# Hyperedge attention in a four-layer graph kernel: score products, closing steps and loads of two chunks issued together

## The chip, the cores and the metric

The kernel runs on one core of a Trainium2 chip. The metric is the device time of one execution in microseconds (us), and lower is better. The figure for a kernel is the median of several executions.

The core has five engines with instruction queues of their own, each worked off in order: PE (matrix multiplication; its weight loads, PEld, run beside the multiplications), DVE (element-wise work and reductions), ACT (activation functions), POOL (element-wise work, and here mostly the issuing of DMAs) and SP (which only issues DMAs). They meet at semaphores. [...]

## The reference, cut to what matters

Four graph layers are computed one after the other on `x` of shape (8, 2048, 64), each as `x = x + layer(relu(layernorm(x)))`. The change touches the end of the first, an attention over hyperedges. When that end begins there are two candidates for every node, `industry` (neighbours averaged through `adj`) and `g` (hyperedges averaged by attention), and a softmax over the two mixes them:

```python
def attn_scores(f):
    return jnp.tanh(f @ fcW + fcb) @ av
...
pair = jnp.stack([industry, g], axis=2)
coefs2 = jax.nn.softmax(attn_scores(pair), axis=-1)
out = jnp.einsum('bnk,bnkf->bnf', coefs2, pair)
```

A softmax over two scores is a sigmoid of their difference d, and a sigmoid is `0.5 + 0.5*tanh(d/2)`. So the kernel computes `tanh(fcW' industry + fcb) - tanh(fcW' g + fcb)`, multiplies by `av`, takes `tanh(d/2)`, and blends `g + (tanh(d/2) + 1) * (industry - g)/2`. The second layer, an attention over neighbours, follows at once.

## The kernel before, in words

`four_layers` (line 2299) runs `layer0`, then `Layer1`, then layers 2 and 3. The last part of `layer0` (lines 1500 to 1593), here called **the mixing stage**, is what the change touches. Two batches lie side by side on the 128 partitions, so there are four pairs p of batches, and each has 2048 nodes in four chunks of 512 columns: 16 chunks, numbered 0 to 15. Chunks 0 to 3 belong to p = 0.

The steps of chunk i, and the engine of each:

- `fetch(i)` (line 1520): SP loads `industry` of the chunk into one of eight buffers `iv`. Chunk i takes the buffer of chunk i - 8, and so waits until that chunk is finished and stored.
- `first(i)` (1525) and `second(i)` (1528): through `scores` (1509) PE multiplies `fcW` with `industry` (named `iv`) or with `g` (named `hn` in the trace, `gT` in the code) into a two-bank PSUM tile `pf`. ACT takes the tanh of it into an SBUF tile `th_s`. There are two `pf` tiles, so a product has to wait for the tanh of the product two before it. `second` also has DVE turn `iv` into the half difference of the candidates.
- `differ(i)` (1534): DVE subtracts the two tanh tiles (128 by 1024).
- `third(i)` (1537), "the score product": PE multiplies `Av` with that difference into a one-bank tile `pd`, and ACT takes the tanh in place. There are two `pd` tiles, so the product of a chunk needs `fourth` of the chunk two before it to have read its tile.
- `fourth(i)` (1545), "the closing step": DVE blends into `iv`. For p = 0 two more additions on DVE follow (1552, 1553), and SP stores the sum; for the other p, POOL issues a DMA that adds `iv` to `x1_dram`. After the last chunk of each p, `late_tile` has POOL load one more tile of the adjacency matrix.

The order on each engine is written out by hand. `InOrder` (line 624) and `kit.mm` with `kit.strict` (735) keep each instruction where the program puts it on its engine. The loop from line 1572 runs i from 0 to 17; turn i of it issues, in this order, `first(i + 1)`, `second(i + 1)`, `third(i - 1)`, `differ(i)`, `fourth(i - 2)` and `fetch(i + 6)`, each where its chunk exists.

Between them, `near(engine, i)` issues pieces of the next layer for p = 0 (`first_neighbours`, line 1667, with its plan from line 1771). The ones that matter here are the means (`centre`, two chunks in turns 4 and 8, PE), the subtraction of them (`centred`, turns 5 and 9, DVE), `clipped` on DVE, `maps` (turns 6, 7, 10 and 11, PE, into tiles `ph`), the 13 small DVE operations `guess`, `newton` and `scored` (turns 12 and 13), `rows` (turns 14 and 15, PE, into `pb`), and four products `edge` (turns 16 and 17, DVE, 128 by 1024 each, named `pt`). With these `edge` tiles the attention over neighbours starts: `Layer1.attend` (line 1821), whose DVE products are on line 1813 and whose PE products are named `o` and `dn`.

In the trace, instructions issued through `kit.mm` have line 737, and those through `InOrder` have line 632, so they are told apart by tile.

## Time and profile before

| | us |
|---|---|
| median of 3 runs (lowest, highest) | 1865.65 (1864.99, 1867.82) |
| the profiled execution | 1868.58 |
| its span | 1866.8 |
| PE busy in the span | 1826.9 (98%) |
| DVE busy | 1196.0 (64%) |
| ACT busy | 476.1 (26%) |
| POOL busy | 317.9 (17%) |
| first product of the mixing stage (PE, `pf`) | at 351.46 |
| first DVE product of `attend` (line 1813) | at 421.95 |

All times "at" are counted from the start of the span. The profiled execution took 1.8 us more than its span, and 2.9 us more than the median. In a timeline a row gives its start, its duration, the engine, the line, the operation, what it writes and reads, the shape, and how many instructions were merged; in square brackets stands how long the engine had been idle before it and what ended that. In a list of waits a row gives who waited for whom, the sum in us, how often, and the longest. In a table by stage a row gives the stretch, its length, the busy time of each engine (with its number of instructions), the granted PE clock as a share of full speed, and the load of the DMA engines.

### The profile page before, as it was taken

Reading aid. Unit: us, or ns where it says so; the run is one execution under the profiler, and the core shown is the slowest. Engines: PE = TensorE matmul, PEld = TensorE weight load, DVE = VectorE, ACT = ScalarE, POOL = GpSimd, SP = SyncE. Lnnn points to the kernel's source line nnn. Section 1 sums busy time; section 2 is a strip of 40 time slices with the busy share of each in tenths; the row PEclk is TensorE's granted clock in tenths of the full one; section 3 lists DMA queues with packets and bytes.
Section 4 is the critical chain, followed back from the end, with each engine's and each line's share of the span. In section 5 each row is a group of like instructions: output and inputs, shape, how many; then the busy total and the mean of one; then the engine's idle time right before and its main releaser. Section 6 shows DMA issues by size and latency. Waiting matters only on the chain.

```text
span 1866.8 us, 26248 instructions
## 1 busy us (share of the span) xinstructions
PE 1826.9 (98%) x10358; PEld 1137.9 (61%) x10358; DVE 1196.0 (64%) x1881; ACT 476.1 (26%) x1088; POOL 317.9 (17%) x437
## 2 busy tenths in 40 slices
PE   7999999899999999999999999999999999999997
PEld 7878767343333333477765577855677755777653
DVE  6778799789999998932446722367533276424465
ACT  5433455672222221121301112201112101113000
POOL 3212487120000000000112200012100021101122
PEclk9999999999999999999999999999999999999998
DMA  6677494492222222142101022100122011221000
GB/s 189 167 211 221 126 280 127 118 215 75 60 54 56 51 57 58 46 104 64 51 10 31 22 70 62 34 24 25 44 63 63 12 29 29 62 57 51 5 20 13
DMA packets 84390, 142.61 MB, mean 76 GB/s; under 512 B 31752, under 2 KB 32008, under 8 KB 81520
## 3 DMA queue, kind: packets, MB, share of 16 engines
q1 hardware_dynamic: 62832, 79.59, 14.6%
q0 software_dynamic: 21200, 58.03, 12.8%
q10 hardware_dynamic: 224, 3.22, 0.5%
q8 instruction: 83, 1.36, 0.3%
q14 instruction: 51, 0.42, 0.1%
HBM read 106.85 MB, written 37.09 MB: 77 GB/s over the span
## 4 chain that ended last, share of the span: by engine, by line
PE 50%; issue 10%; DMA 2%; POOL 2%; DVE 1%; POOLq 0%; ACT 0%; SPq 0%; DVEq 0%
PE acc L737 31%; PE u L737 14%; PE py L737 2%; PE pv L737 1%; PE tx L744 1%; PE tv L744 1%; POOL fold L2284 1%; DMA den<-d_dram 0%; DMA W3f<-in_L_gnn_weight 0%; DMA xd<-e 0%; DMA d_dram<-ds 0%; POOL ot L2285 0%; PE tp L744 0%; DVE pt L1813 0%; POOL ot L2286 0%
## 5 line engine op out<-in xcount | busy, mean ns | idle before, releaser
L737 PE MATMUL acc<-aT,parts 128*128 128x512 f32 x1664 | 430.5, 404 | 0.0
L737 PEld LDWEIGHTS acc<-aT,parts 128*128 128x128 f32 x1664 | 305.6, 188 | 87.0 <-issue 27.7
L2272 DVE TENSOR_TENSOR pr<-u,embf 128x512 f32<-128x512 f32 x256 | 170.6, 687 | 125.4 <-PE u L737 118.4
L737 PE MATMUL o<-pt,hS 128*32 128x512 f32 x2048 | 247.4, 593 | 2.7 <-DVE pt L1813 1.4
L737 PE MATMUL u<-W3f,y 64*128 64x512 f32 x1024 | 241.2, 589 | 0.0
L1813 DVE SCALAR_TENSOR_TENSOR pt<-R,wd,aT 128x1024 f32<-128x1024 f32 x188 | 230.0, 1276 | 8.0 <-DMA R<-r_dram 4.9
L737 PEld LDWEIGHTS u<-W3f,y 64*128 64x128 f32 x1024 | 99.9, 187 | 119.8 <-issue 119.8
L737 PEld LDWEIGHTS o<-pt,hS 128*32 128x32 f32 x2048 | 75.1, 110 | 148.8 <-issue 123.8
L737 PE MATMUL dn<-pt,vd 128*32 128x512 f32 x1024 | 135.0, 593 | 0.0
L737 PE MATMUL u<-W3f,v 64*128 64x512 f32 x512 | 134.3, 600 | 0.0
L2284 POOL TENSOR_TENSOR fold<-fold 128x256 f32<-128x256 f32 x64 | 51.2, 801 | 485.1 <-DVE fold L2283 485.1
L2066 DVE TENSOR_TENSOR yb<-py,cb_f 128x512 f32<-128x512 f32 x32 | 22.1, 691 | 157.9 <-PE py L737 157.9
L1106 PE MATMUL acc<-at,Y 128*128 128x512 f32 x384 | 103.4, 405 | 0.0
L737 PE MATMUL acc<-aTl,parts 128*128 128x512 f32 x384 | 97.5, 396 | 0.0
L2163 POOL TENSOR_TENSOR bq<-bq,xp 128x512 f32<-128x512 f32 x16 | 20.7, 1293 | 421.2 <-ACT xp L2088 421.2
L2276 DVE TENSOR_TENSOR pr<-pr 128x512 f32<-128x512 f32 x128 | 88.1, 688 | 2.2
L1813 DVE SCALAR_TENSOR_TENSOR pt<-R,wd,aTl 128x1024 f32<-128x1024 f32 x64 | 79.3, 1280 | 8.7 <-PE dn L737 3.9
L737 PEld LDWEIGHTS acc<-aTl,parts 128*128 128x128 f32 x384 | 72.1, 188 | 17.0
L737 PEld LDWEIGHTS u<-W3f,v 64*128 64x128 f32 x512 | 54.8, 186 | 45.1 <-issue 33.4
L737 PEld LDWEIGHTS dn<-pt,vd 128*32 128x32 f32 x1024 | 38.3, 110 | 70.1 <-issue 55.5
L1106 PEld LDWEIGHTS acc<-at,Y 128*128 128x128 f32 x384 | 68.8, 189 | 12.7 <-issue 0.3
L2088 ACT COPY xp<-tx 128x512 f32<-128x512 f32 x25 | 14.7, 588 | 202.9 <-PE tx L744 202.9
(376 smaller groups left out, 2708.1 us busy)
## 6 DMA issues: line engine op xcount, KB each, us to landing
at<-in_adjT POOLq DMA_DIRECT2D x32, 512.0 KB, 5.3
raw<-in_adjT SPq DMA_DIRECT2D x64, 256.0 KB, 3.3
aT<-in_adjT POOLq DMA_DIRECT2D x12, 1024.0 KB, 8.0
xp<-xd SPq DMA_DIRECT2D x45, 256.0 KB, 3.0
R<-r_dram SPq DMA_DIRECT2D x14, 512.0 KB, 3.8
hhi<-hi_dram POOLq DMA_DIRECT2D x18, 235.1 KB, 4.8
hlo<-lo_dram POOLq DMA_DIRECT2D x18, 235.1 KB, 5.0
hi_dram<-hi SPq DMA_DIRECT2D x16, 264.0 KB, 3.1
```

The costliest lines, as they stand in the source:

```text
L737: one = self.nc.tensor.matmul(*args, **kw)
L744: one = self.nc.tensor.transpose(dst, src, self.ident[0:k, 0:k])
L1106: mm(acc[p], Y[h][:, m, p, :], at[:, k, :], start=m + h == 0, stop=m == NT - 1 and h == 1)
L1813: V.scalar_tensor_tensor(pt, R, w, a.bitcast(FP), op0=OP.max, op1=OP.mult)
L2066: nc.vector.tensor_tensor(yb, py, bias[:, None, :].to_broadcast([P, 4, P]), op=OP.add)
L2088: nc.scalar.copy(xp, tx.rearrange("p k n -> p (k n)"))
L2163: nc.gpsimd.tensor_add(bq, bq, xp)
L2272: nc.vector.tensor_tensor(a, u[h], emb[:, i, 8 * w : 8 * w + 8, None].to_broadcast([P, 8, F]), op=OP.mult)
L2276: nc.vector.tensor_add(pr[h], pr[h], a)
L2284: nc.gpsimd.tensor_add(fold[:, :, 0:2, :], fold[:, :, 0:2, :], fold[:, :, 2:4, :])
```

## The change

Three steps of the loop are issued for two chunks at a time, on turns of one parity:

- `third` of chunks i - 2 and i - 1 is issued on even turns i, one right after the other, and ahead of `first` and `second` of that turn. The even chunk comes one turn later than before; the odd chunk stays in its turn but moves ahead of the products of `first`, `second` and of the pieces `PE0`.
- `fourth` of chunks i - 3 and i - 2 is issued on odd turns. The even chunk comes one turn later, with its store or its accumulating DMA; the odd chunk stays in its turn.
- `fetch` of chunks i + 5 and i + 6 is issued on odd turns; chunks 8, 10, 12 and 14 come one turn later.

No instruction is added or taken away, and no tile changes its size or its number of buffers.

```diff
             near("DVE", i)
+            if i and i % 2 == 0 and i <= len(chunks):
+                third(i - 2)
+                third(i - 1)
             if 0 < i < len(chunks) - 1:
                 first(i + 1)
             if i < len(chunks) - 1:
                 second(i + 1)
             near("PE0", i)
-            if 0 < i <= len(chunks):
-                third(i - 1)
             near("PE", i)
             if i < len(chunks):
                 differ(i)
-            if i > 1:
+            if i > 1 and i % 2:
+                fourth(i - 3)
                 fourth(i - 2)
-            if 0 < i and i + 6 < len(chunks):
-                fetch(i + 6)
+            for k in (i + 5, i + 6):
+                if i % 2 and 6 < k < len(chunks):
+                    fetch(k)
             near("V2", i)
             near("ACT", i)
```

## The prediction

> **What bounds the kernel now.** I read the page first: PE is busy 98% of the span, so what delays PE delays the end unless PE makes it up later. The chain of waits does not help here: its earliest piece is at 668 us, and the mixing stage lies at 351 to 422 us. So I asked for the busy time of each engine by stage, ending with most of the attention behind the stage:

> ```profile
> 366.00:390.00 24.00, 22.68 (x104) 9.72 (x102) 20.51 (x34) 15.63 (x22) 4.12 (x5) 1.00 0.70 158
> ...
> 404.00:422.00 18.00, 15.87 (x98) 7.14 (x100) 16.71 (x32) 11.43 (x18) 4.85 (x6) 1.00 1.00 201
> 470.00:815.00 345.00, 342.94 (x3068) 125.50 (x3061) 305.83 (x271) 74.32 (x189) 22.15 (x32) 1.00 0.23 56
> ```

> The columns are stretch, length, then busy time of PE, PEld, DVE, ACT and POOL. In the last row PE is idle for 2.1 of 345 us. A delay handed to that stretch is not made up there. In the mixing stage two engines are nearly full, PE and DVE, so the order in which they wait for each other decides. The list of waits between 351 and 422 us shows the two that matter:

> ```profile
> PEld pf L737 <- ACT th_s L632: 8.8, 15, 1.0
> PEld pd L737 <- DVE iv L632: 7.8, 8, 1.8
> ```

> A projection waits for the tanh that frees a `pf` tile, a score product for the closing step that frees a `pd` tile. Most of both is weight loads that hide under the multiplications.

> **The steady turn.** From the timeline, one turn of p = 0:

> ```profile
> 361.06 1.22 DVE L632 TENSOR_TENSOR th_s<-th_s 128x1024 f32<-128x1024 f32 x1
> 361.19 1.08 PE L737 MATMUL pd<-th_s,Avf 128*64 128x512 f32 x4
> ...
> 362.20 0.68 DVE L632 SCALAR_TENSOR_TENSOR iv<-pd,iv 128x512 f32<-128x512 f32 x1
> 362.20 1.13 PE L737 MATMUL pf<-iv,fcWf 64*128 64x512 f32 x4
> ...
> 363.17 1.02 PE L737 MATMUL pf<-hn,fcWf 64*128 64x512 f32 x4
> ...
> 364.12 1.08 PE L737 MATMUL pd<-th_s,Avf 128*64 128x512 f32 x4
> ...
> 364.25 0.69 DVE L632 SCALAR_TENSOR_TENSOR iv<-hn,iv 128x512 f32<-128x512 f32 x1
> ```

> PE goes score product, `first`, `second` with starts 1.01, 0.97 and 0.95 apart: 2.93 a turn. The score product stands between the pairs of projections, and while PE makes it, ACT catches up with its tanh. DVE: `differ` takes 1.14 to the next start, a closing step of p = 0 takes 362.20 to 364.25 = 2.05.

> **What the change saves.** Score products also run side by side at the end of the stage today:

> ```profile
> 415.02 1.94 PE L737 MATMUL pd<-th_s,Avf 128*64 128x512 f32 x8
> ...
> 416.88 1.05 PE L737 MATMUL o<-pt,hS 128*32 128x512 f32 x4
> ```

> Two take 416.88 - 415.02 = 1.86; apart they take 2 x 1.01, and each costs the product before it another 0.1. So a pair saves at most 0.24, and eight pairs 1.9 us.

> **What it costs.** Two chains get longer. First, `first`, `second`, `first`, `second` now stand together, with two `pf` tiles. The start of the stage has that pattern today:

> ```profile
> 353.86 2.13 PE L737 MATMUL pf<-hn,fcWf 64*128 64x512 f32 x8 [0.42 <-ACT th_s L1517]
> ...
> 355.04 2.12 ACT L632 ACTIVATE th_s<-pf,fcbf 128x1024 f32<-128x1024 f32 x2 [0.22 <-PE pf L737]
> 356.20 1.13 PE L737 MATMUL pf<-iv,fcWf 64*128 64x512 f32 x4 [0.21 <-ACT th_s L632]
> ...
> 357.21 1.13 PE L737 MATMUL pf<-hn,fcWf 64*128 64x512 f32 x4
> ...
> 357.40 0.68 DVE L632 SCALAR_TENSOR_TENSOR iv<-hn,iv 128x512 f32<-128x512 f32 x1
> ...
> 358.00 1.22 DVE L632 TENSOR_TENSOR th_s<-th_s 128x1024 f32<-128x1024 f32 x1
> ```

> From a pair to the next is 356.20 - 353.86 = **2.34** (not 1.92), because the third product waits for the first tanh. DVE's `iv` step follows a `first` by **1.20**, `differ` that step by **0.60**.

> Second, and dearer: all of it is in order, and the score products of turn e + 2 now stand at the head of PE's queue. They need `pd` tiles that are freed by the closing steps of turn e + 1, and those stand on DVE behind `iv` and `differ` of turn e + 1. From a closing step to the product it releases I take **0.74**:

> ```profile
> 374.76 0.68 DVE L632 SCALAR_TENSOR_TENSOR iv<-pd,iv 128x512 f32<-128x512 f32 x1
> ...
> 375.50 1.08 PE L737 MATMUL pd<-th_s,Avf 128*64 128x512 f32 x4 [0.61 <-DVE iv L632]
> ```

> While PE waits there, the next `first` is held behind the score products, and with it ACT and then DVE: nothing runs ahead, and the wait comes back every two turns. I sum it from `first(k)` to `first(k + 2)`, k odd:

> - F3: `second(2)` at 357.21, + 0.95; the pair's other product needs `differ(1)` (358.00 + 1.22 + 0.06); + 1.01 = 360.29. Before 359.28: **+1.01**.
> - F3 to F5: 2.34 + 1.20 + 0.60 + 1.14 + 2.05 (all of `fourth(0)` before `fourth(1)`) + 0.74 + 1.01 = 9.08. Before 365.13 - 359.28 = 5.85: **+3.23**.
> - F5 to F7: as before it, but 1.92 + 1.92 (the means, 386.90 to 388.82) = 3.84 stand where 2.34 stood: 10.58. Before 7.77: **+2.81**.
> - F7 to F9: PE has enough of its own: twice `first`, `second` (1.92) and `maps` (382.10 to 383.98 = 1.88), plus 1.88 for the score products = 9.48, and DVE is through in time (3.80 + 1.20 + 0.60 + 1.14 + 0.74 = 7.48 against 7.60). Before 11.08, with two stalls behind DVE that the later start now covers: **-1.60**.
> - F9 to F11: 3.84 + 1.20 + 0.60 + 1.14 + 0.74 + 0.87 (the other product of the pair) + 1.01 = 9.40. Before 7.76: **+1.64**.
> - F11 to F13: like F7 to F9, 9.48. Before 9.62: **-0.14**.
> - F13 to F15: 1.20 + 0.60 + 1.14, then `guess`, `newton`, `scored` (404.89 to 407.71 = 2.82), then 0.60 + 1.14 + 0.74 + 0.87 + 1.01 = 10.12. Before 5.86: **+4.26**.
> - F15 to the first DVE product of `attend`: tanh of `second(15)` 2.19 later, done 1.11 after that, + 0.08, `differ(15)` 1.14, two closing steps 1.20: the first `edge` after 5.72; then four `edge` (1.20 each) and two closing steps = 6.00. Together 11.72. Before 421.95 - 407.22 = 14.73, where PE's `rows` stood ahead of two score products: **-3.01**.

> The sum is +8.2: that product starts at about 430.2 instead of 421.95. The first `o` on PE moves as far, because it waits for the same `edge` products.

> **What costs nothing, and its cover.** Tanh of the scores on ACT (0.51 each) falls into the pause of the projections; uncovered it would be 0.5 a round. Loads: the tightest is chunk 14. Its buffer is freed by POOL's accumulating DMA of chunk 6, issued at about 397.2 instead of 387.88, 6.1 to landing in the list of DMAs; the load then takes 5.4 (median; longest 9.3): 408.7, at worst 412.6. `first(14)` is due at 408.34 + 2.34 = 410.7, but DVE's small operations leave it until about 413. Uncovered it costs up to 1.9. SP's stores of p = 0 go out in twos ahead of loads due 12 us later: nothing.

> **Clock.** Ahead of the stage PE once waited 3.37 us, and the next to last column, the granted clock, fell:

> ```profile
> 344.00:345.00 1.00, 0.00 (x0) 0.01 (x1) 1.00 (x3) 0.00 (x0) 0.00 (x0) 0.79 0.00 0
> 345.00:346.00 1.00, 0.98 (x2) 0.46 (x3) 0.47 (x1) 0.00 (x0) 0.00 (x0) 0.50 0.00 0
> ```

> It stood at 0.50 until 348, 3 us with work. The sum has one pause as long, ahead of the score products of turn 14 (about 4.0 us, behind DVE's small operations); the others are below 2. Losing half of 3 us there is +1.5; not losing it is 0. I take 0, since a wait in the middle of work may fall either way, and keep 1.5 for the range.

> [...]

> **Rivals.**
> 1. *Not slower: the waits stay hidden.* PE would gain the switches, -1.9 us: 1863.7. It decides if closing steps end before PE reaches the score products. For it: PE itself idled only 1.6 us for `pd` today. Against: the chain above leaves PE 1.7 to 4 us early, four rounds out of six.
> 2. *The attention takes half of it back*: +4.1, 1869.8. For it: DVE has 39 of 345 us free there. Against: PE has 2.1.
> 3. *Clock and a late load on top*: +8.2 + 1.5 + 1.9 = 11.6, 1877.3.
> 4. *The order on the engines does not become what the loop says*: 1865.7. Against: these steps are issued in program order on every engine.

> **The numbers.** Against the profiled execution: 1868.58 + 8.2 = 1876.8, span 1875.0. Against the median, 2.9 lower: **1873.9**. Each row may be off by a tenth or two over some forty steps: 1.5 either way. Chances: forecast 0.65, rival 3 0.18, rival 2 0.10, rival 1 0.04, rival 4 0.03. Range from rival 2 to rival 3: 1869.7 to 1877.6. A difference of 0.2% (3.7 us) is what a measurement of this kernel can tell from none. Rival 2 lies at that edge, rivals 1 and 4 inside it: same 0.11, slower 0.88, faster 0.01.

> **What would show it.** Right: first `attend` product on DVE near 430; score products in eight groups of eight records; `pd` waiting for DVE `iv` on PE itself, about 2 us a time, in the rounds F3, F5, F9 and F13, and no such wait in F7 and F11. F15 near 418.5. Wrong: score products that start with no idle PE before them, or a start of the attention at 430 with an end that is not 8 us later.

## The result and the profile after

| | before | after |
|---|---|---|
| median of 6 runs (lowest, highest), us | 1866.63 (1864.99, 1870.70) | 1877.17 (1875.19, 1879.70) |
| ratio of after to before, with its 95% interval | | 1.0051 [1.0040, 1.0063] |
| the profiled execution | 1868.58 | 1879.70 |
| its span | 1866.8 | 1877.8 |
| first `pf` product of the mixing stage, at | 351.46 | 350.91 |
| first DVE product of `attend`, at | 421.95 | 433.53 |
| from the one to the other | 70.49 | 82.62 |
| rest of the span behind it | 1444.85 | 1444.3 |

The change makes the kernel slower by about half a per cent (0.0051 x 1866.63 = 9.5 us, interval 7.5 to 11.8; the two medians lie 10.5 apart). The last three rows say where: the mixing stage is 12.1 us longer in the profiled execution, which is the slowest of the six, and all that follows is as long as before.

The table by stage of the kernel after (stretch, length, busy time of PE, PEld, DVE, ACT and POOL, then granted clock), with the two stretches of the stage and most of the attention:

```profile
366.00:390.00 24.00, 20.38 (x92) 8.60 (x88) 18.19 (x29) 13.32 (x19) 0.96 (x2) 0.93 0.41 131
404.00:422.00 18.00, 13.90 (x58) 5.30 (x56) 11.91 (x30) 10.08 (x16) 4.92 (x6) 0.83 1.04 216
433.00:815.00 382.00, 379.37 (x3443) 139.59 (x3444) 347.75 (x312) 84.70 (x232) 23.50 (x34) 1.00 0.23 57
```

In the first two rows PE and DVE both lost busy time: neither is the bound any more, they wait for each other. And the clock, 1.00 in both stretches before, is 0.93 and 0.83. In the third row PE is still idle for only 2.6 of 382 us, so the attention had no room to give the delay back.

The list of waits of the kernel after, between 351 and 430 us:

```profile
PEld pd L737 <- DVE iv L632: 16.7, 8, 4.5
...
PE pd L737 <- DVE iv L632: 10.5, 6, 3.7
...
PEld pf L737 <- ACT th_s L632: 7.1, 8, 1.2
```

Score products (`pd`) wait 10.5 us on PE itself for the closing steps, in six waits; before there were two, 1.6 us in all. One round of it, from the timeline of the kernel after:

```profile
363.08 1.13 PE L737 MATMUL pf<-hn,fcWf 64*128 64x512 f32 x4
363.25 0.69 DVE L632 SCALAR_TENSOR_TENSOR iv<-hn,iv 128x512 f32<-128x512 f32 x1 [0.52 <-PE pf L737]
...
363.86 1.22 DVE L632 TENSOR_TENSOR th_s<-th_s 128x1024 f32<-128x1024 f32 x1
364.99 0.68 DVE L632 SCALAR_TENSOR_TENSOR iv<-pd,iv 128x512 f32<-128x512 f32 x1
...
365.73 1.08 PE L737 MATMUL pd<-th_s,Avf 128*64 128x512 f32 x4 [1.52 <-DVE iv L632]
...
367.78 1.86 PE L737 MATMUL pd<-th_s,Avf 128*64 128x512 f32 x4 [0.97 <-DVE iv L632]
...
369.57 2.00 PE L737 MATMUL pf<-iv,fcWf 64*128 64x512 f32 x4
```

PE is through with `second` and has nothing it may start: the score product at the head of its queue needs the `pd` tile that the closing step of 364.99 reads, and that step stands on DVE behind `iv` and `differ` of the same turn. Only after both score products comes the next `first`. The last product and the last score product took 2.00 and 1.86 us, where the same shapes take 1.13 and 1.08 elsewhere: the granted clock was 0.50 from 367.95 to 371.36.

### The profile page after: what moved, and what is told of

The parts are those of the page before. It is cut to its first block, busy times and chain, and to the rows that moved or that the text cites. A ratio compares the mean times of both kernels' runs of the same rounds, so it can differ in the third digit from the quotient of the medians.

```text
span 1877.8 us, 26247 instructions
## 1 busy us (share of the span) xinstructions
PE 1830.8 (97%) x10358; PEld 1147.1 (61%) x10358; DVE 1196.5 (64%) x1881; ACT 476.7 (25%) x1088; POOL 317.5 (17%) x437
## 4 chain that ended last, share of the span: by engine, by line
PE 49%; issue 10%; DMA 2%; POOL 2%; DVE 1%; POOLq 0%; ACT 0%; SPq 0%; DVEq 0%
PE acc L737 31%; PE u L737 14%; PE py L737 2%; PE pv L737 1%; PE tx L744 1%; PE tv L744 1%; POOL fold L2287 1%; DMA den<-d_dram 0%; DMA xd<-e 0%; DMA W3f<-in_L_gnn_weight 0%; DMA d_dram<-ds 0%; PE tp L744 0%; POOL ot L2288 0%; DVE pt L1816 0%; POOL ot L2289 0%
## 5 line engine op out<-in xcount | busy, mean ns | idle before, releaser
L737 PE MATMUL acc<-aT,parts 128*128 128x512 f32 x1664 | 430.5, 404 | 0.0
L737 PEld LDWEIGHTS acc<-aT,parts 128*128 128x128 f32 x1664 | 305.7, 188 | 87.0 <-issue 27.7
L737 PE MATMUL o<-pt,hS 128*32 128x512 f32 x2048 | 245.4, 593 | 1.4 <-DVE pt L1816 1.3
L737 PE MATMUL u<-W3f,y 64*128 64x512 f32 x1024 | 243.0, 589 | 0.0
L737 PEld LDWEIGHTS u<-W3f,y 64*128 64x128 f32 x1024 | 101.8, 187 | 118.6 <-issue 118.6
L737 PEld LDWEIGHTS o<-pt,hS 128*32 128x32 f32 x2048 | 79.0, 110 | 142.2 <-issue 112.3
L737 PE MATMUL u<-W3f,v 64*128 64x512 f32 x512 | 136.1, 601 | 0.0
L737 PE MATMUL dn<-pt,vd 128*32 128x512 f32 x1024 | 133.8, 593 | 0.2 <-DVE iv L632 0.2
L737 PE MATMUL acc<-aTl,parts 128*128 128x512 f32 x384 | 97.5, 396 | 0.0
L737 PEld LDWEIGHTS u<-W3f,v 64*128 64x128 f32 x512 | 55.6, 186 | 45.1 <-issue 33.4
L737 PEld LDWEIGHTS acc<-aTl,parts 128*128 128x128 f32 x384 | 72.1, 188 | 17.0
L737 PEld LDWEIGHTS dn<-pt,vd 128*32 128x32 f32 x1024 | 40.1, 110 | 68.3 <-issue 49.9
L1106 PEld LDWEIGHTS acc<-at,Y 128*128 128x128 f32 x384 | 68.8, 188 | 12.7 <-issue 0.3
```

Source lines behind the costliest of these rows:

```text
L737: one = self.nc.tensor.matmul(*args, **kw)
L1106: mm(acc[p], Y[h][:, m, p, :], at[:, k, :], start=m + h == 0, stop=m == NT - 1 and h == 1)
```

## The experiments

Each kernel ran beside the kernel before on the same chip; a ratio is to that kernel's runs. "Stage" is the time from the first `pf` product to the first DVE product of `attend` in the one profiled execution, "rest" what follows it in the span, "waits" the sum of PE's own waits for a score product, and "low clock" the stretches of the stage at a granted clock of 0.50.

| run | median | ratio [95%] | stage (minus 70.49) | rest | waits | low clock in the stage |
|---|---|---|---|---|---|---|
| after, first profile | 1877.17 | 1.0051 [1.0040, 1.0063] | 82.62 (+12.13) | 1444.3 | 10.5 | 367.95 to 371.36, 415.73 to 422.56 |
| after, again | 1875.97 | 1.0052 [1.0038, 1.0066] | 80.20 (+9.71) | 1444.0 | 10.5 | 415.99 to 419.41 |
| scores paired | 1874.66 | 1.0050 [1.0037, 1.0063] | 78.12 (+7.63) | 1444.4 | 7.7 | 411.30 to 414.71 |
| closing paired | 1878.37 | 1.0066 [1.0053, 1.0079] | 83.64 (+13.15) | 1444.9 | 11.7 | 415.73 to 422.56 |
| loads paired | 1867.23 | 1.0004 [0.9995, 1.0013] | 70.52 (+0.03) | 1444.5 | 1.6 | none |
| scores behind | 1866.20 | 1.0001 [0.9992, 1.0010] | 70.26 (-0.23) | 1444.8 | 0.6 | none |
| scores between | 1869.97 | 1.0018 [1.0009, 1.0027] | 72.99 (+2.50) | 1444.5 | 3.1 | none |
| PE kept busy | 1875.03 | 1.0043 [1.0030, 1.0056] | 78.66 (+8.17) | 1446.4 | 3.9 | none |
| closing first | 1882.38 | 1.0076 [1.0059, 1.0094] | 83.14 (+12.65) | 1444.7 | 10.1 | three times 3.41 |
| behind from chunk 4 | 1864.39 | 0.9995 [0.9986, 1.0004] | 68.77 (-1.72) | 1445.1 | 0 | none |
| order by the sum | 1868.62 | 1.0010 [1.0001, 1.0019] | 73.17 (+2.68) | 1445.8 | 1.5 | 402.72 to 406.13 |
| busy ahead | 1870.95 | 1.0016 [1.0005, 1.0026] | 70.49 (0.00) | 1445.2 | 1.6 | none |
| order and busy | 1873.06 | 1.0035 [1.0021, 1.0049] | 73.16 (+2.67) | 1446.2 | 1.5 | 403.50 to 406.92 |

### One part of the change alone

**Scores paired** (closing steps and loads as before):

```diff
+            if i and i % 2 == 0 and i <= len(chunks):
+                third(i - 2)
+                third(i - 1)
             if 0 < i < len(chunks) - 1:
...
-            if 0 < i <= len(chunks):
-                third(i - 1)
```

> Only the score products are paired, at the head of even turns; closing steps and loads stay one a turn as before. Theory (the product at the head of PE's queue waits for a chain through DVE): the first product of a pair finds its tile free since the turn before, the second still waits for a closing step behind differ, so a plain round is 2.34 + 1.20 + 0.60 + 1.14 + 0.74 + 1.01 = 7.03 long instead of 5.85, and the rounds with maps cost nothing: +5 to +7 us against the kernel before, some 2 us less than the whole change. Rival (the paired closing steps, with tiles held a turn longer, are what costs): within 1 us of the kernel before.

The stage grew by 7.63, more than the 5 to 7 expected, and the whole time by about as much as with all of the change, not 2 us less. Four waits for `pd` on PE, 1.96, 1.81, 0.66 and 3.27 us, sit where the prediction's chain puts them; behind the 3.27 the clock was 0.50 for 3.41 us, which the expectation had not priced.

**Closing paired** (score products and loads as before):

```diff
-            if i > 1:
+            if i > 1 and i % 2:
+                fourth(i - 3)
                 fourth(i - 2)
```

> Only the closing steps are paired, on odd turns; score products and loads stay one a turn as before. Theory: each score product still has two projections (1.92 us) between it and the turn before, which covers most of the wait; only the rounds of p = 0 and the last closing step are late: +1.5 to +2 us against the kernel before. Rival (the paired closing steps cost): +6 to +9 us.

The expectation failed: this half alone costs as much as the whole, or more. From its timeline:

```profile
361.69 1.13 PE L737 MATMUL pf<-iv,fcWf 64*128 64x512 f32 x4
...
364.61 0.68 DVE L632 SCALAR_TENSOR_TENSOR iv<-pd,iv 128x512 f32<-128x512 f32 x1
...
365.34 1.08 PE L737 MATMUL pd<-th_s,Avf 128*64 128x512 f32 x4 [1.67 <-DVE iv L632]
```

In every second turn the score product needs a closing step that now comes a turn late, in that same turn behind `iv` and `differ`. From `first` to the product it is 1.20 + 0.60 + 1.14 + 0.74 = 3.68 by the steps of the prediction (365.34 - 361.69 = 3.65 here), and PE has only two projections of work, 1.92, to fill it. The wait of 1.67 came five times, and one of 3.31 behind DVE's small operations. My sum for this kernel had left this wait out. So the two halves do not add up: the stage is 7.63 and 13.15 longer with one of them, 12.13 with both. I read it so that each alone makes a closing step late for a score product, and together they share that wait.

**Loads paired**:

```diff
-            if 0 < i and i + 6 < len(chunks):
-                fetch(i + 6)
+            for k in (i + 5, i + 6):
+                if i % 2 and 6 < k < len(chunks):
+                    fetch(k)
```

> Only the loads are issued two at a time, on odd turns; score products and closing steps as before. Theory (loads are covered): same time, within 1 us of the kernel before, and no projection waits for a load. Rival (chunks 8, 10, 12 and 14 arrive late): +1 to +4 us, with PE waiting for iv.

Nothing that the runs can tell, in the stage (+0.03) or in the time (1.0004).

### The place of the pair in PE's queue

**Scores behind**: all of the change, the pair of score products moved to behind `second` and `PE0` (the edit is shown against the kernel after).

```diff
             near("DVE", i)
-            if i and i % 2 == 0 and i <= len(chunks):
-                third(i - 2)
-                third(i - 1)
             if 0 < i < len(chunks) - 1:
...
             near("PE0", i)
+            if i and i % 2 == 0 and i <= len(chunks):
+                third(i - 2)
+                third(i - 1)
             near("PE", i)
```

> The whole change, but the paired score products stand behind first, second and the pieces PE0 of the same even turn instead of ahead of them. The order on PE is again projections, projections, score products, so the switches and the two adjacent pairs of projections are kept; only what stands between turn e + 1 and the products differs (1.92 us of PE work). Theory: the wait is covered and the whole loss goes: -1 to +0.5 us against the kernel before, and no low clock in the stage. Rival (the four projections in a row wait for ACT, or the pairing as such costs): +3 us or more remains.

The whole loss is gone: ratio 1.0001, stage -0.23, clock 1.00. In its list of waits of PE the score products have nearly none:

```profile
PE pd L737 <- DVE iv L632: 0.6, 2, 0.4
```

Pairs, projections standing together and closing steps in twos are all still there. What costs is that the pair stands ahead of products that could run.

**Scores between**: all of the change, the pair moved to between `first` and `second` (against the kernel after).

```diff
             near("DVE", i)
+            if 0 < i < len(chunks) - 1:
+                first(i + 1)
             if i and i % 2 == 0 and i <= len(chunks):
                 third(i - 2)
                 third(i - 1)
-            if 0 < i < len(chunks) - 1:
-                first(i + 1)
             if i < len(chunks) - 1:
                 second(i + 1)
```

> The whole change, but the pair of score products stands between first and second of the even turn. One projection (0.97) and not two lie in front of it. Theory: the closing step that frees the tile is through 1.20 + 0.60 + 1.14 + 0.74 = 3.68 after the first of the odd turn, PE gets there after 0.97 + 0.95 + 0.97 = 2.89, so 0.8 a round is left of the wait and first has run ahead of it: +1.5 to +3.5 us against the kernel before, between the whole change and the products behind both. Rival (it only matters whether the products come first or last): as the whole change or as the kernel before.

+2.50 in the stage, 1.0018 in the time. One projection ahead of the pair hides a part of each wait: five are left, 3.1 in all, the longest 1.0.

**Closing first**: all of the change, the two closing steps moved from behind `differ` to the head of DVE's turn.

```diff
+            if i > 1 and i % 2:
+                fourth(i - 3)
+                fourth(i - 2)
             near("DVE", i)
...
             if i < len(chunks):
                 differ(i)
-            if i > 1 and i % 2:
-                fourth(i - 3)
-                fourth(i - 2)
```

> The whole change, but the two closing steps stand at the head of DVE's odd turn, ahead of the pieces DVE, of the iv step and of differ. Theory (the loop is projections, tanh, differ, score product, next projections; the closing steps are only its last link): the second product of the pair needs differ of the turn just before, which now stands behind two closing steps (4.1 us for p = 0, 1.2 for the others), so the wait changes its releaser but not its length: +7 to +9.5 us against the kernel before. Rival (it is the place of the closing steps behind differ that costs): below +4 us.

The rival, that the place of the closing steps behind `differ` is to blame, falls: the wait stays, under another name. In its timeline:

```profile
371.11 1.81 PE L737 MATMUL pd<-th_s,Avf 128*64 128x512 f32 x4 [3.41 <-DVE th_s L632]
```

Now `differ` (`th_s`) stands behind the closing steps, and the second product of the pair needs it. The loss is larger than my theory said, +12.65 in the stage and 14.2 by the ratio against 7 to 9.5: behind each of the pauses of 3.41, 3.27 and 2.75 us the clock was 0.50 for 3.41 us. The expected wait came; the clock was missing from the sum.

### The clock

**PE kept busy**: all of the change, and six products whose result nobody reads, queued ahead of the waiting pair in the four rounds.

```diff
             near("PE", i)
+            for _ in range({3: 1, 5: 1, 9: 1, 13: 3}.get(i, 0)):
+                mm(one.ps.tile([P, CW], FP, tag="ln", name="idle"), kit.avg, gT[3][:, cols(0)], start=True, stop=True)
```

> The whole change, with six extra products (128 by 512, 0.86 us each, results not used) issued on PE in the pauses ahead of the score products: one in turns 3, 5 and 9 and three in turn 13. They fit into the pauses, so the order and the waits stay. Theory (the low clock is an extra of 1.5 to 4 us on top of the chain's 8.2): the granted clock stays at 1.00 in the stage and the kernel is 1 to 2.5 us faster than the whole change, +7 to +8.5 against the kernel before. Rival A (the low clock is most of the loss): within 3 us of the kernel before. Rival B (the low clock costs nothing since PE has time): as the whole change, +9 to +10.

More work, and a shorter stage: 78.66, and +8.17 is what the prediction's rows add up to without a clock term. In the whole time the gain is not shown: the ratio is 1.0043, and its interval overlaps those of the change (1.0051 and 1.0052). In this profile the rest, which no edit touches, is 1.6 longer than before; what made it so is not shown. In the timeline of the kernel after, the longest pause, and in that of this run, the added products that fill most of it:

```profile
417.51 3.68 PE L737 MATMUL pd<-th_s,Avf 128*64 128x512 f32 x8 [3.68 <-DVE iv L632]
```

```profile
409.79 3.49 PE L737 MATMUL idle<-hn,avg_f 128*128 128x512 f32 x6
413.54 1.94 PE L737 MATMUL pd<-th_s,Avf 128*64 128x512 f32 x8 [0.26 <-DVE iv L632]
```

The pair behind them takes 1.94 at a clock of 1.00, not 3.68.

**The change again**, to see how much of its loss differs from one execution to another:

> The changed kernel once more, for its interval beside these runs and a second profile. Theory (8.2 us of waits plus 1.5 to 4 us of low clock): +9 to +11 us against the kernel before; from the third first product to the first product of attend about 74 us plus the low clock, with PE at half clock behind the pause ahead of product 12 and, in some executions, behind that ahead of product 2. Rival (the first profile's low clock was a chance of that execution): stage of 74 us, +7 to +8.5 us.

All waits are the same to a hundredth, 10.5 in all. But the clock fell to 0.50 only once, for 3.41 us instead of three times that, and the stage is 2.4 shorter. From its timeline, the longest pause and the products behind it:

```profile
414.86 2.60 PE L737 MATMUL pd<-th_s,Avf 128*64 128x512 f32 x8 [3.68 <-DVE iv L632]
417.39 2.08 PE L737 MATMUL pf<-iv,fcWf 64*128 64x512 f32 x4
```

What differs is where the low stretches lie. Between 330 and 437 us, all low stretches of all fourteen profiles (before, after and the twelve here) are 3.41 or 6.83 long, and in one execution they start a multiple of 3.41 apart (367.95 and 415.73 in the first profile: 47.78 = 14 x 3.413). Cut on that grid, the profiles before and after have the clock at 1.00 or at 0.50 in every window from 3 to 1860 us, at 0.50 in 3 of 544 and in 5 of 545. Here is the table by stage, cut in this way: the kernel after, first profile (length, PE busy first, clock third from the end):

```profile
364.54:367.95 3.41, 1.25 (x6) 0.37 (x8) 3.31 (x6) 1.41 (x2) 0.00 (x0) 1.00 0.00 0
367.95:371.36 3.41, 3.41 (x8) 0.88 (x8) 1.20 (x2) 0.58 (x1) 0.00 (x0) 0.50 0.62 188
...
412.32:415.73 3.41, 1.51 (x8) 0.30 (x4) 3.00 (x15) 2.94 (x6) 0.00 (x0) 1.00 1.11 210
415.73:419.14 3.41, 1.63 (x4) 0.53 (x6) 3.11 (x5) 0.00 (x0) 1.39 (x3) 0.50 0.83 173
419.14:422.56 3.42, 3.42 (x10) 1.08 (x8) 0.00 (x0) 1.16 (x2) 0.91 (x2) 0.50 1.13 116
```

And the run again, where the same two pauses of 1.52 and 0.97 are split by the grid's line at 364.79:

```profile
361.38:364.79 3.41, 1.89 (x10) 0.42 (x8) 2.86 (x5) 2.71 (x3) 0.00 (x0) 1.00 0.00 0
364.79:368.20 3.41, 2.44 (x10) 0.58 (x12) 3.23 (x5) 0.93 (x2) 0.00 (x0) 1.00 0.21 77
...
412.58:415.99 3.41, 1.13 (x6) 0.48 (x8) 3.38 (x6) 0.43 (x4) 0.89 (x2) 1.00 1.04 217
415.99:419.41 3.42, 3.42 (x10) 0.99 (x8) 0.24 (x1) 1.16 (x2) 1.41 (x2) 0.50 1.02 144
```

In these two profiles the windows in which PE was busy for 1.25, 1.51 and 1.13 us were followed by one at half clock; after those with 1.89 and 2.44 the clock stayed at 1.00. In the window from 415.73 the pause still ran, PE worked 1.63, and a second window at half clock followed. Cut in this way, the fourteen profiles have 413 windows between 330 and 437 us. Of 378 at full clock, the 24 with PE busy for 0.44 of the window or less were followed by half clock, the 354 with 0.51 or more were not. Of 35 at half clock, the 11 with 0.84 or less were followed by another, the 24 with 0.86 or more by full clock. There is no exception in this stretch. In others there are. A window at 207.5 us of the kernel after, with PE busy for 0.84 of it, was followed by half clock; in the run "closing first" the half clock that began there lasted three windows, though PE was busy for 0.95 of the first and all of the second. And near 9 us of the profiles before and after PE paused for 3.40 and 3.06 us, was busy for 0.60 and 0.35 us of a window, and the clock stayed at 1.00. So the busy share of the trace goes with the clock in this stretch, but it is not all that decides it.

### Looking for a better order

**Behind from chunk 4**: the order before up to turn 4, then the pairs with the score products behind `second`.

```diff
-            if 0 < i <= len(chunks):
+            if 0 < i < 5:
                 third(i - 1)
+            if 5 < i <= len(chunks) and i % 2 == 0:
+                third(i - 2)
+                third(i - 1)
...
-            if i > 1:
+            if 1 < i < 6:
                 fourth(i - 2)
+            if i > 6 and i % 2:
+                fourth(i - 3)
+                fourth(i - 2)
```

> The kernel before with two edits: from chunk 4 on the score products are paired behind the projections of even turns, and the closing steps paired on odd turns; chunks 0 to 3 (three DVE operations in a closing step) and the loads stay as before. Theory: pairing saves the switches (up to 0.24 for each of six pairs = 1.4) and takes PE's waits for products 5 and 13 away (0.6 and 1.0 in the profile before): -1 to -3 us against the kernel before, the end of the stage 2 us earlier. Rival (the saved switches are lost to the wait of the third projection in a row for the first tanh, 0.4 a round): within 1 us of the kernel before.

The stage is 1.72 shorter, and no wait of a score product on PE is left (1.6 us before). The time, 0.9 us lower by the ratio and 1.9 by the medians, cannot be told from no change: 0.9995 [0.9986, 1.0004].

**Order by the sum**: a place for each score product and each closing step, worked out with the durations of the prediction. An excerpt; each entry is a turn and a place in it:

```diff
+        T3 = [(1, 0), (2, 2), (4, 0), (5, 2), (5, 2), (7, 2), (7, 3), (9, 2), ...
+        T4 = [(2, 1), (4, 0), (4, 2), (6, 3), (7, 0), (8, 1), (9, 1), (10, 0), ...
```

> The kernel before with every score product and closing step put, within its one or two possible turns, where the sum of the prediction (same rows, same waits) makes the stage shortest; loads follow the closing step that frees their buffer. Score products stand behind one or both projections wherever a closing step is awaited. Theory (the stage is set by these in-order waits, and the sum has them right): from the third first product to the first product of attend 61.5 us instead of 65.75, so -3 to -5 us against the kernel before. Rival (before is already at the limit of PE and DVE in this stage): within 1.5 us.

Failed, +2.68 instead of a gain. Its timeline shows what the sum had left out, the loads:

```profile
385.14 0.86 POOL L632 DMA_DIRECT2D xd<-iv x1 [2.88 <-issue]
...
402.11 1.52 PE L737 MATMUL pf<-iv,fcWf 64*128 64x512 f32 x4 [2.92 <-DMA iv<-ind_dram]
```

The closing step of chunk 5 had moved back. The accumulating DMA that frees the buffer of chunk 13 was issued at 385.14 instead of 383.08, though the stage began 1.40 earlier. The load that had to wait for it (the loads of this stage took 3.0 to 9.4 from issue to landing, median 6.2) was not there when `first(13)` was due: that started at 402.11, 16.97 behind the issue. The clock was 0.50 behind that pause too, for 3.41 us, and the first score product waited 1.54 for `differ`.

**Busy ahead**: the kernel before, with four products whose result nobody reads in front of the mixing stage, to keep the clock up over its 3.37 us pause.

```diff
             if j == last + 2:
+                for _ in range(4):
+                    idle = ps.tile([P, SLOTS], FP, tag="pa", name="idle", bufs=2)
+                    mm(idle, kit.avg, slot, start=True, stop=True)
                 done(LT - 4)
```

> The kernel before with four extra products (128 by 384, about 0.64 us each, results not used) in the pause of 3.37 us that PE has ahead of the mixing stage, after which the clock stood at 0.50 for 3 us. Theory (a pause without PE work costs by the low clock that follows): the clock stays at 1.00 and the stage begins 1 to 2 us earlier: -1 to -2 us. Rival (PE has slack there): same time, within 0.5 us.

Failed, 1.0016. From its timeline:

```profile
344.39 2.03 PE L737 MATMUL pgs<-mix,S 128*114 128x512 f32 x2 [3.37 <-DVE gn L632]
346.21 3.38 PE L737 MATMUL idle<-slot,avg_f 128*128 128x384 f32 x8
```

The waiting product was already ahead of them in PE's queue. So the pause stayed, and the added products ran behind it, the first 1.3 us of them at half clock (it lasted until 347.47). The stage itself is 70.49, as before.

**Order and busy**, both edits together:

> The edits of the two runs before together. Theory: they lie one behind the other and add up: -4 to -7 us against the kernel before. Rival: the one takes what the other would have given, -3 to -4 us.

Both losses are there: the stage is that of "order by the sum" (73.16), and the time is above that of either, 1.0035.

## Why the prediction was right, and where it was off

Forecast 1873.9, measured 1877.17, slower, and inside the range, 0.4 below its upper end. That end holds 1.9 for a late load that did not come, so that the median lies inside is in part luck. Some of the distance is the kernel before, whose median is now 1866.63 and not 1865.65; against it 8.2 were forecast and 9.5 measured by the ratio, whose interval (7.5 to 11.8) holds both. So it is the profiles, not the total, that show which terms were right. The rows of the sum against the first profile of the change, where F2 is the start of `first(2)`, and so on:

| row | predicted | measured | products at half clock in this row |
|---|---|---|---|
| F2 to F3 | 4.09 | 4.08 | |
| F3 to F5 | 9.08 | 9.84 | 1.86 instead of 1.08 |
| F5 to F7 | 10.58 | 11.42 | 2.00 instead of 1.13 |
| F7 to F9 | 9.48 | 9.47 | |
| F9 to F11 | 9.40 | 9.36 | |
| F11 to F13 | 9.48 | 9.47 | |
| F13 to F15 | 10.12 | 11.83 | 3.68 instead of 1.94 |
| F15 to `attend` | 11.72 | 12.41 | 1.83 instead of 1.13 |

- **The chain** (pair at the head of PE's queue, closing step behind `iv` and `differ`): shown. The four rows without low clock are right to 0.04. The waits are in rounds F3, F5, F9 and F13 as predicted (1.52 + 0.97, 1.67 + 0.97, 1.67, and 3.68 against "about 4.0"), and none in F7 and F11. "Scores behind" takes away the place alone, and the loss goes. Whether more `pd` tiles would have spared the wait was not tried.
- **The clock term** is the step that was mis-sized: priced at 0, with 1.5 as its bound. The four differences add up to 4.0; in the run again it fell once, and the products behind the pause took 2.60 and 2.08 instead of 1.94 and 1.13: 1.6. "PE kept busy" takes it away and leaves 8.17 of 8.2. The reason for 0, that a wait in the middle of work may fall either way, was not borne out by the pause of 3.68: in both profiles the clock was 0.50 behind it, for 6.83 and for 3.41 us, and it was 0.50 behind all the others of 2.75 to 3.41 in the stage of the runs. It fits the two short pauses (1.52 and 0.97), with 0.50 for 3.41 us behind them in the first profile and 1.00 in the second; I had left them out of the clock altogether. The pause of 3.37 us ahead of the stage, from which I took the bound, spoke for a price already: of the 3.41 us up to 344.59 PE was busy for 0.47, and the clock was 0.50 from there to 348.00. Pricing a pause as long at 0 was too kind to the change.
- **Loads at nothing**: shown alone by "loads paired" (+0.03). The margin that I gave chunk 14 held, with the accumulating DMA issued at 398.19 instead of about 397.2: `first(14)` waited only 0.42, for a tanh. But my worst case was too mild. I took the median of 6.1 for that DMA, and in the profile before the very one of chunk 6 (issued at 387.88) took 9.4 to land; here it took 6.7. What a late load costs, "order by the sum" shows.
- **Rival 1** (not slower) falls: six waits, 10.5 us. The waits stay hidden with the pair behind the projections, and "scores behind" is level with the kernel before; but the 1.9 that pairs were to save do not show even there (stage -0.23).
- **Rival 2** (the attention takes half back) falls: the rest of the span is 1444.0 to 1446.4 in all fourteen profiles, with stages from 68.8 to 83.6.
- **Rival 3** (clock and a late load): its clock came, and more of it; its load did not. Its price, 11.6, is near the measured loss for a reason that is half its own.
- **Rival 4** falls: score products stand in pairs on PE, as written.
- **The total**: 8.2 and the clock, 4.0, less 0.1 in the other rows, is 12.1 for the first profile; with 1.6 it is 9.7 for the run again. Over all executions the ratio says 9.5. That the executions of the change scatter (1875.03 to 1880.30) because the low stretches lie differently is argued from these two profiles, not shown for the others. The granted clock of each whole execution goes the same way: 0.992 in the slowest of both runs (1879.70, 1880.30), 0.994 and 0.996 in the fastest (1875.19, 1875.03); it does not say where in the execution the clock was lost. Open, too, is whether "behind from chunk 4" is faster: its gain is smaller than the runs can tell.
- **Two slips of the sum** that decide nothing: by its own rows F13 is at 408.31, not 408.34, and a pair saves 2 x 1.01 - 1.86 + 0.1 = 0.26, not 0.24.

## What to carry to other kernels

In a queue worked off in order, ask of the instruction that you move to the head not how long it takes but when its last releaser ends, and where that releaser stands in its own engine's queue; here pairs were free behind work that could run (stage -0.23), and dear ahead of it (+12.13). Where a sum has pauses of PE as long as the longer ones here, add the clock to it: behind each pause of 2.75 to 3.68 us in the stage the clock was 0.50 for 3.41 or 6.83 us, and behind two short ones close together (1.52 and 0.97) it was so, for 3.41 us, in one execution of two. An order that is worked out on paper needs the buffers' way round in it (closing step, store, next load), or it moves the wait to a DMA; work meant to fill a pause must stand ahead of the waiting instruction.
